# Three changes of tile form and order around the attention scores of a hybrid block

## The chip, the cores and the metric

The kernel runs on one core of one Trainium2 chip. Its time is the device time of one execution in microseconds, given as the median over runs. A profile is one execution taken by the hardware profiler, with every instruction of every engine: TensorE (PE, with its weight loads PEld), VectorE (DVE), ScalarE (ACT), GpSimd (POOL), and the DMA queues, which SP and others issue.

## The reference

Input x is 8 batches of 512 tokens of 1024 features, all float32. Four residual steps follow each other, each on a layer norm of x:

```python
x = x + attn_a(layernorm(x))   # 32 heads of 32: softmax(q k^T / sqrt(32)) v, then the output product
x = x + ffn(layernorm(x))      # dense 1024 x 1024, rows and tokens gated by clusters that are hit
x = x + attn_b(layernorm(x))   # 4 heads of 256, sigmoid scores, causal
x = x + ffn(layernorm(x))      # the same dense layer again
```

The change touches only the first step, `attn_a`:

```python
qkv = x @ attn_qkvw + attn_qkvb
scores = einsum('bhqd,bhkd->bhqk', q, k) * scale
probs = softmax(scores)
ctx = einsum('bhqk,bhkd->bhqd', probs, v)
return ctx @ attn_ow + attn_ob
```

## The kernel before

`softmax_attention` works through 64 units `n`: 8 batches (`b`) by 8 groups (`g`) of 4 heads. The 4 heads of a group have 32 features each and so fill the 128 partitions. A unit has these steps, each cut in 4 tiles of 128 queries or keys:

- `rows_step` (L863 to L872) computes the scores by query of the next unit, one matmul for each head on its 32 partitions, and VectorE takes the negative maximum of every query (`nmax`, L872).
- `split_max` splits -max into three bf16 parts, and `turn_max` (L884 to L892) turns them with an identity on TensorE; ScalarE copies the result to `shift`, in bf16.
- `keys_step` (L894 to L906) computes the scores by key. It first adds up k times q (L900) and then ones times `shift` (L903) in the same PSUM tile, which subtracts the maximum; ScalarE's exponential (L905) reads that tile into `pT`.
- `values_step` (L918 to L929) multiplies `pT` with v in column tiles of 32, and `normalize` (L931) divides by the sums.

The scores by query and by key share one PSUM tile `sc` of four banks, one bank for each head, in a pool with a single buffer. So each waits until VectorE or ScalarE has read the one before.

What fills TensorE between these steps are the *fillers*: the projections to q, k and v of the unit after next (`project_pieces`), the output products of the batch before (`out_pair`), and transposes and logits for the step that follows. They lie in one queue (`Filler`); each piece has a weight, and `take` runs a share of what is queued. The order of all of TensorE's instructions is thus written out when the program is built, and nothing is reordered by a scheduler. The loop of a unit is

```python
for i in range(TPB):
    rows_step(n + 1, i)
    between()
    if i == 0:
        turn_max(n)
        between()
    keys_step(n, i)
    # i == 0: values_step(n - 1, 1), logits, normalize(n - 1);  i == 2: values_step(n, 0)
    between(False, HD_A if i in (0, 2) and n > 0 else 2 * HD_A)
```

A filler's products go through `product` (L550), which cuts the 128 columns of the stationary operand in column tiles of `width[0]`. `between` sets that width: 64, or 32 where attention values, which use tiles of 32 columns, come just before. `turn_max` and the second step of the cluster logits call `product` too. The first four `rows_step` calls stand ahead of the loop, among products of full width.

A matmul's tile form is written as rows*columns: 32*128 is a tile of 32 rows of the array and all its columns, 128*64 one of all rows and half the columns. Tiles of one form that do not overlap can work side by side.

Of the kernel before, what the change touches and what calls it, by code (L numbers as in the profile page):

```python
# [22 lines left out]
P = 128  # L23
# [6 lines left out]
HEADS_A, HD_A = 32, 32  # L30
# [376 lines left out]
def softmax_attention(tc, cst, stage, filler, clusters, pools, dr, late, args):  # L407
# [11 lines left out]
    nc, small, ps_m = tc.nc, stage.small, stage.ps_m  # L419
# [128 lines left out]
    width = [P]  # L548

    def product(out, lhsT, rhs, **flags):  # L550

        for j in range(P // width[0]):
            cols = ts(j, width[0])
            nc.tensor.matmul(out[cols], lhsT[:, cols], rhs, **flags)  # L554

    first_w = {}
# [36 lines left out]
    def first_pieces(n):  # L593
# [4 lines left out]
        def qk(t, c):  # L598
            def go():
                if c == 0:  # L600
                    st["acc"] = ps_m.tile([P, S], F32, tag="mm", name="mm")
                product(
                    st["acc"], first_w[t, g, c // half][:, c % half, :], xTs[0][:, c, :],
                    start=(c == 0), stop=(c == NC - 1),
                )
                if c == NC - 1:
                    o = st["qk"[t]] = qkpool.tile([P, S], F32, tag=f"qk{t}", name=f"qk{t}_{n}")
                    bias = qkvb_s[:, t * NC + g : t * NC + g + 1]
                    if t == 0:
                        nc.vector.tensor_scalar(o, st["acc"], bias, None, ALU.add)  # L610
                    else:
                        nc.scalar.activation(o, st["acc"], AF.Identity, bias=bias)

            return go

        def v(i, k):
            def go():
                if i == 0 and k == 0:
                    st["acc"] = ps_m.tile([P, TPB, P], F32, tag="mm", name="mm")
                for c in range(half):  # L620
                    product(
                        st["acc"][:, i, :], xTs[0][:, k * half + c, ts(i, P)], first_w[2, g, k][:, c, :],
                        start=(k == 0 and c == 0), stop=(k == 1 and c == half - 1),
                    )
                if i == TPB - 1 and k == 1:
                    st["v"] = vpool.tile([P, TPB, P], F32, tag="v", name=f"v_{n}")
                    nc.scalar.copy(st["v"], st["acc"])

            return go
# [21 lines left out]
    def project_pieces(n):  # L651
# [9 lines left out]
        def qk(k, c0):  # L661
            def go():
                if c0 == 0:
                    st["acc"] = ps_m.tile([P, 2 * P], F32, tag="mm", name="mm")
                for c in (c0, c0 + 1):
                    product(
                        st["acc"], weights.tiles[base + EARLY.index(k)][:, c, :], left(k)[:, c, :],
                        start=(c == 0), stop=(c == half - 1),
                    )
                if c0:  # L670
                    if k == 0:
                        for t in range(2):
                            st["qk"[t]] = qkpool.tile([P, S], F32, tag=f"qk{t}", name=f"qk{t}_{n}")
                    q, kk = st["q"], st["k"]
                    bias = [qkvb_s[:, t * NC + g : t * NC + g + 1] for t in range(2)]
                    gather(nc, k, st["acc"], q[:, lo], kk[:, lo], q[:, hi], kk[:, hi], bias, early=True)
                    weights.done(base + EARLY.index(k))

            return go
# [183 lines left out]
    def rows_step(n, qt):  # L863

        st = state[n]
        if qt == 0:
            st["nmax"] = small.tile([P, TPB, GH], F32, tag="nmax", name=f"nmax_{n}")
        sc = ps_s.tile([P, GH, S], F32, tag="sc", name="sc")
        for h in range(GH):
            rows = ts(h, HD_A)  # L870
            nc.tensor.matmul(sc[:, h, :], st["q"][rows, ts(qt, P)], st["k"][rows, :], start=True, stop=True)  # L871
        nc.vector.tensor_reduce(st["nmax"][:, qt, :], sc, AX.X, ALU.max, negate=True)  # L872

    def split_max(n):
# [19 lines left out]
    def keys_step(n, kt):  # L894

        st = state[n]
        sc = ps_s.tile([P, GH, S], F32, tag="sc", name="sc")
        for h in range(GH):
            rows = ts(h, HD_A)
            nc.tensor.matmul(sc[:, h, :], st["k"][rows, ts(kt, P)], st["q"][rows, :], start=True, stop=False)  # L900
        for h in range(GH):
            rows = ts(h, HD_A)
            nc.tensor.matmul(sc[:, h, :], cst.ones_h[rows, :], st["shift"][rows, :], start=False, stop=True)  # L903
        pT = ptp.tile([P, GH, S], F32, tag="pT", name=f"pT_{n}_{kt}")
        nc.scalar.activation(pT, sc, AF.Exp, scale=SCALE_A)  # L905
        st["pT", kt] = pT  # L906
# [40 lines left out]
        nc.vector.tensor_tensor(out, st["av"], rden, ALU.mult)  # L947
        nc.scalar.activation(out, out, AF.Identity, bias=qkvb_s[:, 2 * NC + g : 2 * NC + g + 1])

    places = [0]  # L950

    def between(sides=True, form=2 * HD_A):


        if sides:
            for _ in range(-(-len(side) // places[0])):
                side.popleft()()
            places[0] -= 1
        width[0] = form
        filler.take()  # L960

    def mix_tile(near, wait):
        norm, logits = tiles.popleft()(blocks=wait)
        filler.mix(norm[:2], 0 if near else 2, 2 if near else 5)
        filler.mix(norm[2:], 9 if near else 14, 3)
        if wait:
            waiting.append(logits)
        else:
            filler.mix(logits, 16 if near else 22, 4)
# [25 lines left out]
    for i in range(TPB):  # L995
        rows_step(0, i)
        run(pieces[6 * i : 6 * i + (6 if i < 3 else len(pieces))])
# [4 lines left out]
    for n in range(units):  # L1002
# [33 lines left out]
        for i in range(TPB):  # L1036
            if n + 1 < units:
                rows_step(n + 1, i)
            if i == 0 and n > 0:
                sum_step(n - 1, TPB - 1)  # L1040
# [4 lines that stand above are left out]
            if i == TPB - 1:  # L1045
                sum_step(n, i - 1)
            keys_step(n, i)
            if i == 1:
                sum_step(n, i)
            if i == 0 and n > 0:  # L1050
                values_step(n - 1, 1)
                if ready:
                    by_cluster, by_token = ready.popleft()
                    run([by_cluster])
                    filler.mix([by_token], 6, 1)
                normalize(n - 1)
            if i == 2:
                values_step(n, 0)
            between(False, HD_A if i in (0, 2) and n > 0 else 2 * HD_A)
# [268 lines left out]
def block_body(tc, long, dr, args, out):  # L1328
# [7 lines left out]
    def pools(stack, side):  # L1336
# [12 lines left out]

    late = [[] for _ in range(TPB)]  # L1350
    attention = softmax_attention(
        tc, cst, stage, filler, hits1, (pools(a_outer, left), pools(a_inner, right)), dr, late,
        (x, xT_in, qkvw, qkvb, ow, ob),
# [319 lines left out]
```

## Time and profile before

| | |
|---|---|
| time, median of 3 runs | 3769.76 us (3768.65 to 3769.84) |
| time of the profiled execution | 3769.5 us |
| its span, first to last instruction | 3767.8 us |
| granted TensorE clock, mean | 0.997 |
| mean DMA rate | 159 GB/s |
| scores by query, L871 | 2048 matmul records, 291.9 us busy |
| scores by key, L900 and L903 | 2048 and 1024 records, 292.9 and 101.1 us busy |
| attention stage with the changed code | from about 40 to about 2560 us |

The span is what the trace shows; the time of an execution has under 2 us around it. Busy time of TensorE counts a record from its start to an end that is modelled, so neighbouring records overlap: the starts of records are firmer than their lengths. A float32 matmul leaves two matmul records and two weight loads, a bf16 one leaves one of each.

### The profile page before, as it was taken

What the parts mean: (1) busy time and instruction counts of PE and PEld (TensorE: products, weight loads), DVE (VectorE), ACT (ScalarE), POOL (GpSimd) and SP (SyncE); (2) the same over time, 40 slices, a digit from 0 to 9 for tenths busy, and PEclk for the clock granted to TensorE, in tenths of its full rate; (3) what the DMA queues carried; (4) which work ended last, traced back from release to release, by engine and by line L of the source; (5) the groups of instructions that cost most, each with busy time, mean ns of one, the idle gap of its engine ahead of it and who ended that gap; (6) DMA issues with size and microseconds to landing.
All of it is one profiled execution on the core that took longest, in us unless ns stands there. A gap on an engine that the chain in (4) does not pass through costs nothing.

```text
span 3767.8 us, 72200 instructions
## 1 busy us (share of the span) xinstructions
PE 3716.6 (99%) x30746; PEld 1902.9 (51%) x30746; DVE 2543.7 (68%) x3495; ACT 909.8 (24%) x983; POOL 594.0 (16%) x572
## 2 busy tenths in 40 slices
PE   8999999999999999999999999998999999999999
PEld 4444455554545555555545445443444467764444
DVE  4777676777667667766766767665788845556656
ACT  1222222222222222222222322222111144430000
POOL 1222111111111111111111111111000045530000
PEclk9999999999999999999999999999999999999999
DMA  5335444645655455465455444346566667763332
GB/s 171 115 127 168 142 137 146 194 137 150 188 144 152 149 160 168 132 194 151 134 179 163 141 148 123 118 155 235 159 178 173 170 190 233 226 210 128 134 128 101
DMA packets 728625, 598.29 MB, mean 159 GB/s; under 512 B 322152, under 2 KB 574064, under 8 KB 728304
## 3 DMA queue, kind: packets, MB, share of 16 engines
q1 hardware_dynamic: 701072, 496.40, 46.0%
q0 software_dynamic: 22912, 81.54, 5.6%
q10 hardware_dynamic: 4320, 15.73, 1.0%
q8 instruction: 243, 3.98, 0.4%
q14 instruction: 78, 0.64, 0.1%
HBM read 459.30 MB, written 134.25 MB: 158 GB/s over the span
## 4 chain that ended last, share of the span: by engine, by line
PE 90%; DVE 5%; DMA 1%; issue 1%; SPq 1%; POOL 0%; ACT 0%; DVEq 0%; POOLq 0%; ACTq 0%
PE mm L554 41%; PE dense L1236 17%; PE sc L900 7%; PE sc L871 7%; PE av L927 6%; PE o L1314 4%; PE csc L1295 3%; PE sc L903 1%; PE logitsT L325 1%; PE den L939 1%; DVE nmax L872 1%; PE tp L277 1%; DVE sum L916 0%; SPq L300 0%; DVE u L142 0%
## 5 line engine op out<-in xcount | busy, mean ns | idle before, releaser
L872 DVE TENSOR_REDUCE nmax<-sc 128x4 f32<-128x2048 f32 x256 | 585.9, 2289 | 294.7 <-PE sc L871 294.7
L905 ACT ACTIVATE pT<-sc 128x2048 f32<-128x2048 f32 x256 | 480.8, 1878 | 1151.8 <-PE sc L903 1146.9
L914 POOL TENSOR_TENSOR sum<-pT,pT 128x1024 f32<-128x1024 f32 x128 | 309.8, 2442 | 766.1 <-ACT pT L905 724.9
L554 PE MATMUL mm<-xT,w 128*64 128x256 f32 (+1 forms) x3736 | 429.0, 383 | 1.2 <-DVE rden L942 1.2
L554 PEld LDWEIGHTS mm<-xT,w 128*64 128x64 f32 (+1 forms) x3736 | 241.8, 135 | 197.1 <-issue 47.1
L554 PE MATMUL mm<-s,w 128*32 128x256 f32 (+1 forms) x3672 | 321.2, 381 | 0.5
L900 PE MATMUL sc<-qk,qk 32*128 32x512 f32 x2048 | 292.9, 641 | 10.5 <-DVE nmax L872 9.8
L916 DVE TENSOR_TENSOR sum<-sum,pT 128x2048 f32<-128x2048 f32 x128 | 291.9, 2280 | 1.0 <-ACT pT L905 1.0
L871 PE MATMUL sc<-qk,qk 32*128 32x512 f32 x2048 | 291.9, 640 | 0.4 <-ACT pT L905 0.3
L142 DVE TENSOR_TENSOR u<-dense,u 128x512 f32<-128x512 f32 x223 | 149.1, 685 | 186.9 <-PE dense L1236 170.2
L554 PEld LDWEIGHTS mm<-s,w 128*32 128x32 f32 (+1 forms) x3672 | 180.4, 122 | 176.0 <-issue 68.0
L554 PE MATMUL mm<-ow,ctxT 128*32 128x512 f32 (+2 forms) x1276 | 246.6, 599 | 0.4 <-DMA ow<-o_T 0.4
L927 PE MATMUL av<-pT,v 128*32 128x512 f32 x2048 | 246.6, 599 | 0.0
L1236 PE MATMUL dense<-sum,s 128*128 128x512 f32 x512 | 232.1, 594 | 2.6 <-DVE s L1183 2.6
L554 PEld LDWEIGHTS mm<-w,xT 128*64 128x64 f32 (+1 forms) x3888 | 197.5, 133 | 57.3 <-issue 44.7
L554 PE MATMUL mm<-w,xT 128*64 128x128 f32 (+1 forms) x3888 | 218.1, 274 | 0.0
L144 DVE SCALAR_TENSOR_TENSOR qk<-mm,qkvb_s,qk 128x256 f32<-128x256 f32 x224 | 107.5, 480 | 130.2 <-PE mm L554 125.1
L1236 PE MATMUL dense<-wT_s,dT_b 128*128 128x512 f32 x384 | 173.1, 598 | 1.7 <-DMA dT_b<-xT 1.7
L554 PE MATMUL mm<-ow,c 128*64 128x512 f32 (+2 forms) x864 | 170.8, 597 | 2.7 <-DMA ow<-o_T 2.7
L1236 PE MATMUL dense<-wT_s,dT_a 128*128 128x512 f32 x384 | 171.0, 593 | 0.0
L554 PE MATMUL mm<-w,s 128*64 128x128 f32 x2688 | 162.5, 274 | 0.0
L1236 PEld LDWEIGHTS dense<-sum,s 128*128 128x128 f32 x512 | 96.4, 190 | 123.4 <-issue 112.1
(231 smaller groups left out, 4504.7 us busy)
## 6 DMA issues: line engine op xcount, KB each, us to landing
w<-in_qkvw SPq DMA_DIRECT2D x252, 256.0 KB, 3.0
ow<-o_T SPq DMA_DIRECT2D x240, 256.0 KB, 3.6
w<-qk_T SPq DMA_DIRECT2D x224, 256.0 KB, 2.7
ow<-in_ow SPq DMA_DIRECT2D x180, 256.0 KB, 3.1
w<-v_T SPq DMA_DIRECT2D x112, 256.0 KB, 2.7
x<-in_x SPq DMA_DIRECT2D x32, 512.0 KB, 5.3
dT_a<-xT SPq DMA_DIRECT2D x32, 512.0 KB, 6.1
x_a<-x SPq DMA_DIRECT2D x32, 512.0 KB, 6.8
```

Source lines behind the costliest of these rows:

```text
L142: nc.vector.tensor_tensor(out, acc, other, ALU.add)
L554: nc.tensor.matmul(out[cols], lhsT[:, cols], rhs, **flags)
L871: nc.tensor.matmul(sc[:, h, :], st["q"][rows, ts(qt, P)], st["k"][rows, :], start=True, stop=True)
L872: nc.vector.tensor_reduce(st["nmax"][:, qt, :], sc, AX.X, ALU.max, negate=True)
L900: nc.tensor.matmul(sc[:, h, :], st["k"][rows, ts(kt, P)], st["q"][rows, :], start=True, stop=False)
L905: nc.scalar.activation(pT, sc, AF.Exp, scale=SCALE_A)
L914: nc.gpsimd.tensor_tensor(st["sum"][:, h, :], st["pT", 0][:, h, :], st["pT", 1][:, h, :], ALU.add)
L916: nc.vector.tensor_tensor(st["sum"], st["sum"], st["pT", kt], ALU.add)
L927: nc.tensor.matmul(st["av"][rows, :], st["v"][:, kt, rows], pT[:, h, :], start=(kt == 0), stop=(kt == TPB - 1))
L1236: nc.tensor.matmul(st["acc"], st["left"][LEFT[k]][:, c, :], self.w[RIGHT[k]][:, c, :], start=(c == 0), stop=(c == half - 1),)
L1295: nc.tensor.matmul(sc[:, AT_OFF[i] : AT_OFF[i] + n], k[:, c, ts(i, P)], xT[:, c, i * P :], start=(c == 0), stop=(c == 1),)
L1314: nc.tensor.matmul(acc[:, j - jj, :], at[:, start : start + P], self.v[b * TPB + i][:, cols], start=(i == 0), stop=(i == j),)
```

## The change

It has three parts. In `rows_step` each head's matmul is cut in two, for 64 queries each, so that the scores by query use tiles of 32 rows by 64 columns, eight to a step. In `keys_step` the ones times `shift` product comes first and opens the accumulation, and k times q comes second and closes it. And each call of `between` puts a 32 in the list `opening` before it takes fillers; the first call of `product` takes it out and cuts its columns in four tiles of 32, all further products have the width as before. The list is cleared at the end of the call, so `turn_max`, which is called between two of them, is not touched.

```diff
     def product(out, lhsT, rhs, **flags):
 
-        for j in range(P // width[0]):
-            cols = ts(j, width[0])
+
+        w = opening.pop() if opening else width[0]
+        for j in range(P // w):
+            cols = ts(j, w)
             nc.tensor.matmul(out[cols], lhsT[:, cols], rhs, **flags)
...
         for h in range(GH):
             rows = ts(h, HD_A)
-            nc.tensor.matmul(sc[:, h, :], st["q"][rows, ts(qt, P)], st["k"][rows, :], start=True, stop=True)
+            for j in range(2):
+                cols = ts(2 * qt + j, P // 2)
+                nc.tensor.matmul(sc[ts(j, P // 2), h, :], st["q"][rows, cols], st["k"][rows, :], start=True, stop=True)
         nc.vector.tensor_reduce(st["nmax"][:, qt, :], sc, AX.X, ALU.max, negate=True)
...
         for h in range(GH):
             rows = ts(h, HD_A)
-            nc.tensor.matmul(sc[:, h, :], st["k"][rows, ts(kt, P)], st["q"][rows, :], start=True, stop=False)
+            nc.tensor.matmul(sc[:, h, :], cst.ones_h[rows, :], st["shift"][rows, :], start=True, stop=False)
         for h in range(GH):
             rows = ts(h, HD_A)
-            nc.tensor.matmul(sc[:, h, :], cst.ones_h[rows, :], st["shift"][rows, :], start=False, stop=True)
+            nc.tensor.matmul(sc[:, h, :], st["k"][rows, ts(kt, P)], st["q"][rows, :], start=False, stop=True)
...
-    places = [0]
+    places, opening = [0], []
 
     def between(sides=True, form=2 * HD_A):
...
         width[0] = form
+        opening[:] = [HD_A]
         filler.take()
+        opening.clear()
```

## The prediction

> **What bounds the kernel now.** I read first the page's busy times, then its chain of work that ended last, then the timeline of TensorE inside the attention stage, and last the weight loads kept apart by shape.
>
> From the page, part 1 (busy time, share of the span, instructions) and part 4 (the chain):
>
> ```profile
> PE 3716.6 (99%) x30746; PEld 1902.9 (51%) x30746; DVE 2543.7 (68%) x3495; ACT 909.8 (24%) x983; POOL 594.0 (16%) x572
> ...
> PE 90%; DVE 5%; DMA 1%; issue 1%; SPq 1%; POOL 0%; ACT 0%; DVEq 0%; POOLq 0%; ACTq 0%
> ```
>
> TensorE is busy 99% of the span and is 90% of the chain. No other engine has to be made faster or kept from being slower: what a stretch of TensorE's stream gains or loses, the span gains or loses. So the question is what lies between the matmuls. The timeline of TensorE over one piece of the attention loop (start, length, line, tiles, tile form, records):
>
> ```profile
> 1508.20 1.14 PE L871 MATMUL sc<-qk,qk 32*128 32x512 f32 x8
> 1509.27 1.95 PE L554 MATMUL mm<-xT,w 128*64 128x256 f32 x16
> 1511.05 0.39 PE L554 MATMUL tpm<-ident_h,parts 128*64 128x128 bf16 x8
> 1511.27 1.90 PE L554 MATMUL mm<-xT,w 128*64 128x256 f32 x16
> 1513.10 1.14 PE L900 MATMUL sc<-qk,qk 32*128 32x512 f32 x8
> 1514.06 0.39 PE L903 MATMUL sc<-shift,ones_h 32*128 32x512 bf16 x4
> 1514.39 1.92 PE L927 MATMUL av<-pT,v 128*32 128x512 f32 x16
> ...
> 1530.43 3.67 PE L554 MATMUL mm<-s,w 128*64 128x256 f32 x32
> 1534.04 1.14 PE L900 MATMUL sc<-qk,qk 32*128 32x512 f32 x8
> ```
>
> The form (128*64) is rows by columns of one tile of the array. An f32 matmul leaves two records, a bf16 one leaves one. The tiles of a form run side by side, so I count in rounds, one record on every tile. Single starts in the trace (1509.537, 1509.753, 1509.969) put rounds of 256 f32 columns 0.216 us apart; rounds of 512 take 0.427, and of 512 in bf16 0.213. What a segment takes beyond its rounds sits at a change of form:
>
> - 128*64 from the scores into the turned maxima, which have the same form: 1511.05 - 1509.27 = 1.78 for 8 rounds (1.726). So entering costs 0.054.
> - 128*64 from the turned maxima into scores: 1513.10 - 1511.27 = 1.83 for 8 rounds. So leaving costs 0.104. Check: 16 rounds with both ends take 1534.04 - 1530.43 = 3.61 = 3.453 + 0.054 + 0.104.
> - 32*128, scores by query: 1509.27 - 1508.20 = 1.07 for 2 rounds of 0.427, over 0.216: the second round starts 0.534 after the first, so 0.107 is entering and 0.109 leaving.
>
> Entering follows the columns of one weight load, which nothing hides there: 0.107 for 128 columns, 0.054 for 64; for 32 the starts of the attention values give 0.026. Leaving is about 0.10 whatever follows. The place that matters most is one of the few where one column form follows another:
>
> ```profile
> 87.55 1.92 PE L927 MATMUL av<-pT,v 128*32 128x512 f32 x16
> 89.40 1.08 PE L554 MATMUL mm<-xT,w_first 128*64 128x512 f32 x4
> 90.31 1.04 PE L554 MATMUL mm<-wv,xT 128*64 128x128 f32 x16
> ```
>
> 89.40 - 87.55 = 1.85 for 4 rounds (1.71): 0.14, as much as where rows change. The last round starts at 88.861 and the next form at 89.403, 0.115 beyond a round, and its second round 0.053 late at 89.883. Four places in the trace leave 32 columns for 64 at this price. Going from 32 to 64 columns is therefore not free.
>
> **The change, part by part**
>
> **1. The first filler product in four column tiles.** Each call of between() with a form of 64 now starts with one product of 32, followed by 64 again. The streaming is the same (half as wide, twice as many side by side). Inserted is one more segment: enter 0.026, leave 0.115, together 0.141 us. The 64-column segment behind it still pays its own 0.054. Going through the trace's records I count 252 such places behind scores by query and 130 behind scores by key or values (the other 126 run at 32 already). 382 x 0.141 = 53.9 us. Behind the turned maxima it is worse: today that stretch goes on in the same form with nothing to pay. There the 64 segment is cut in two: 0.141 + 0.104 + 0.054 = 0.299, x 64 = 19.1. Sum 73.0. At four of these places another form follows anyway, which takes off about 1: **+71.8**. All of it is on TensorE's path; nothing covers it, since the engine waits there for itself. Bounds: above, 73; below, if the second switch were free, the narrower entry would gain 382 x 0.027 = 10 us. The row at 89.40 decides for the upper end.
>
> **2. -max first in scores by key.** Today the f32 weights of k (128 columns) are loaded in the open, 0.107, and the bf16 ones behind them under a running round. Turned round, the ones are loaded in the open and k under the ones' round of 0.213, which is longer than 0.107. The loads of both shapes:
>
> ```profile
> L900 PEld LDWEIGHTS sc<-qk,qk 32*128 32x128 f32 x2048 | 80.2, 183 | 126.8 <-issue 55.9 <-DVE nmax L872 31.8 <-DVE qk L142 14.9
> ...
> L903 PEld LDWEIGHTS <-ones_h 32*128 32x128 bf16 x1024 | 28.9, 93 | 57.7 <-issue 57.7
> L325 PEld LDWEIGHTS logitsT<-nT,cT_s 128*32 128x32 f32 x1024 | 28.3, 110 | 20.8 <-issue 17.3 <-ACT nT L279 3.3
> ```
>
> The mean of one is 183 ns for f32 and 93 for bf16, less than the 110 of a 32-column f32 load, whose entry is 0.026. A load met in the open shows 181 ns, so 88 ns go: 256 x 0.088 = **-22.5**. The Trainium skill, "TensorE: Matmul & The Clock Gate", section "LDWEIGHTS (loading the stationary operand)", lets a load grow with its columns alone (columns / 1.2 in ns): 107 ns for both, and this edit would gain nothing. Its section on Fast Weight Load has 128 non-FP32 weights load about twice as fast as measured: 53 ns, a gain of 13.7. I take the row. Bounds 0 and -24. What is new is that the segment waits for the shift (ScalarE, L892) one f32 part, 0.96 us, earlier. From the end of that cast to the start of L900 there are 0.70 us in nearly every unit; once, at the end of attention, it is 0.17 short. Who releases L900 today:
>
> ```profile
>   DVE nmax L872: 41.6, 46
> ...
>   ACT shift L892: 0.8, 1
> ```
>
> So no wait is added; the buffer of the scores is freed by the same reduction as before, and the exponential behind still starts after the last matmul of the step.
>
> **3. Scores by query in tiles of 32 by 64.** 256 steps go from 4 tiles to 8: 2048 more matmul records, as many loads, the same two rounds. No row shows this form. Entering should be that of 64 columns: -0.053. But records of one round start 0.0067 apart (1508.199, 1508.206, 1508.213, 1508.219), and the last of eight starts 0.047 in, not 0.020: +0.027. Net -0.026 x 256 = **-6.7**. The Trainium skill's same page, section on packing small matmuls, gives about 4 ns per tile; the sum would be -9.5. Bounds: -13.6 (no stagger), +6.9 (the two loads of a row group one after the other), and +218 if the two column tiles of a row group do not run side by side (one more 0.427 per round). The Trainium skill, "TensorEngine Tiling (Array Packing)", section "Available Configurations", lists 32x64 as eight independent tiles, and both splits are seen side by side separately (four 32*128, two 128*64), so I take the first.
>
> Sum: 71.8 - 22.5 - 6.7 = +42.6 on the profiled execution of 3769.5 us (span 3767.8), 0.3 under the median of the runs, 3769.76: **3812**. No DMA, SP or GpSimd instruction is moved; VectorE's reduction starts when the scores end, as now.
>
> **The rivals**
>
> - *Column forms switch freely within one product's accumulation.* The inserted segment then gains 10 instead of costing 72: -10 - 22.5 - 6.7 = -39, 3730, faster. For it: every place that I price is between different products. Against: 89.40 above. It decides below 29.2 / 446 = 0.065 us for each opening, against 0.161 in my sum.
> - *The eight tiles run as two fours.* 42.6 + 218: about 4030. Against it the two splits above; for it only that no trace here has this form.
> - *The weight side gives nothing.* Loads of one row group in turn (+13.6) and no gain from the ones (+22.5): 3848 with both, 3826 or 3835 with one.
> - *The change does not do what it says*: the first filler piece is seldom a product. Then -29, 3740. The records speak against it: each of the 446 places has one.
>
> **How the numbers follow.** My sum with its small variations 0.80, the weight side failing in full 0.06, two fours 0.07, free switching or an opening that does not bite 0.07. The range runs from 3794 (rows and ones at their best ends, some openings cheaper) to 3842 (the ones gain nothing, rows a little more). 0.2%, 7.5 us, is about what a measurement of this kernel can tell from none: faster 0.06, same 0.02, slower 0.92.
>
> **What would show it.** Step 1: 128*32 segments of 8 records (4 tiles, 2 rounds) right behind L871, 0.57 for 256 columns before the 128*64 starts (0.432 + 0.141). Step 2: L903 ahead of L900, from 1.28 to about 1.20 from the first start to the next form. Step 3: L871 with 4096 records and 1.04 to the next form; 1.9 would mean two fours. Records on PE 30746 + 2048 + 446 x 4 = 34578. A 128*32 to 128*64 step without its 0.11, or a wait for the shift, would make me wrong.

## The result, and the profile after

The changed kernel takes 3803.1 us (median of 4 runs, 3801.1 to 3804.3) against 3769.8 for the kernel before: ratio 1.0088, 95% interval 1.007 to 1.0105. It is slower by 33 us; the forecast was 42 us slower. The two profiled spans are 34.8 us apart (3802.6 and 3767.8).

From the page, the same two parts as before: busy times, and the chain that ended last.

```profile
PE 3751.6 (99%) x34594; PEld 1833.6 (48%) x34594; DVE 2544.5 (67%) x3495; ACT 909.7 (24%) x983; POOL 594.1 (16%) x572
...
PE 93%; DVE 3%; DMA 1%; issue 1%; SPq 1%; ACT 0%; POOL 0%; DVEq 0%; ACTq 0%; POOLq 0%
```

TensorE still carries the chain, now 93% of it. Its records went from 30746 to 34594. That is 16 more than the 34578 expected, or four openings at 4 records each: 450 products are opened, not 446, the last four in the last unit, where no scores by query stand ahead. The same piece of the attention loop in TensorE's timeline follows (start, length, line, tiles, form, records). A line of this view takes in all neighbours of one source line and tile name under the form of the first, so x20 here is one product of 8 records at 128*32 and three of 4 records at 128*64:

```profile
1530.30 1.11 PE L875 MATMUL sc<-qk,qk 32*64 32x512 f32 x16
1531.34 2.08 PE L556 MATMUL mm<-xT,w 128*32 128x256 f32 x20
1533.26 0.39 PE L556 MATMUL tpm<-ident_h,parts 128*64 128x128 bf16 x8
1533.58 2.08 PE L556 MATMUL mm<-xT,w 128*32 128x256 f32 x20
1535.60 0.39 PE L904 MATMUL sc<-shift,ones_h 32*128 32x512 bf16 x4
1535.82 1.03 PE L907 MATMUL sc<-qk,qk 32*128 32x512 f32 x8
1536.78 1.92 PE L931 MATMUL av<-pT,v 128*32 128x512 f32 x16
```

Read start to start, beside the piece of before:

| | before | after | difference |
|---|---|---|---|
| scores by query to the next form | 1.07 | 1531.34 - 1530.30 = 1.04 | -0.03 |
| filler, 8 rounds, up to the turned maxima | 1.78 | 1533.26 - 1531.34 = 1.92 | +0.14 |
| turned maxima to the next filler | 0.22 | 1533.58 - 1533.26 = 0.32 | +0.10 |
| filler, 8 rounds, up to scores by key | 1.83 | 1535.60 - 1533.58 = 2.02 | +0.19 |
| scores by key to the attention values | 1.29 | 1536.78 - 1535.60 = 1.18 | -0.11 |

The inserted 32-column segment costs 0.14 behind the scores and 0.29 (0.10 + 0.19) behind the turned maxima. Weight loads, kept apart by shape:

```profile
L907 PEld LDWEIGHTS sc<-qk,qk 32*128 32x128 f32 x2048 | 101.7, 185 | 4.5
...
L875 PEld LDWEIGHTS sc<-qk,qk 32*64 32x64 f32 x4096 | 59.6, 129 | 112.5 <-issue 93.3 <-ACT pT L909 16.9 <-ACT qk L614 1.2
...
L904 PEld LDWEIGHTS <-ones_h 32*128 32x128 bf16 x1024 | 26.2, 91 | 124.9 <-issue 121.2 <-DVE nmax L876 3.6
```

The loads of k (L907) have almost no idle time before them any more, 4.5 us where it was 126.8: they now run under the round of the ones. The ones, a load of 91 ns, stand in the open instead.

For a sum over the whole attention stage I split TensorE's stream of one profiled execution, from start to start up to the last scores, into three parts:

- Rounds at their nominal length, 0.427 us for 512 f32 columns, half of that in bf16, and in proportion for fewer columns. They make 2306.7 us in every kernel here.
- Form changes: each change counted at the price seen in the starts. Entering costs 0.106, 0.053 and 0.0265 for 128, 64 and 32 columns in f32, and 0.013 for the ones. Each further tile of a round adds 0.0067, or 0.0034 with the ones. Leaving costs 0.091 from a form of 32 rows and 0.0955 from one of all rows.
- The rest: late starts, more than 0.03 us behind what rounds and prices give, and a few nanoseconds for each round that has another of its form on either side.

| kernel | median us | form changes | rest | of it late starts |
|---|---|---|---|---|
| before | 3769.8 | 190.8 | 47.6 | 26.0 |
| after | 3803.1 | 230.1 | 43.3 | 24.1 |
| opening only | 3832.9 | 263.1 | 44.9 | 26.0 |
| max first only | 3747.7 | 164.4 | 53.5 | 31.3 |
| 32x64 only | 3765.8 | 184.0 | 50.6 | 29.0 |
| scores only | 3742.7 | 157.7 | 55.0 | 32.9 |
| three openings | 3953.7 | 388.0 | 33.9 | 19.4 |
| none behind the turned maxima | 3788.1 | 211.2 | 46.3 | 26.3 |
| all 32 | 3746.7 | 152.1 | 65.2 | 43.6 |
| full-width opening | 3869.4 | 299.3 | 41.4 | 22.6 |
| rows 32x32 | 3756.3 | 164.6 | 61.2 | 37.2 |
| more filler first | 3773.5 | 157.7 | 85.7 | 63.8 |
| before, light VectorE | 3758.7 | 190.8 | 39.8 | 18.4 |
| scores only, light VectorE | 3728.2 | 157.7 | 41.9 | 20.2 |

The column of form changes is a count times a price, so agreement of a theory with it is no test by itself. Two things test it. The prices hold place by place: in the changed kernel's trace at the 442 places where 64 columns follow 32 without idle time, the next form starts 0.0957 us (median) beyond the last round, nine in ten between 0.0953 and 0.0967. And the rest stays between 34 and 65 in all kernels but one, while form changes range from 152 to 388. The rest is that of one execution each; times of the kernel before alone spread from 3766.3 to 3774.0 over 25 runs, so a difference of 2 us in it may be chance.

After minus before: form changes +39.3, rest -4.3, together +35.0, against 34.8 in the spans. Of the -4.3, 1.9 are late starts; the other 2.4 are the few nanoseconds of rounds, which the rounds at the ends of the added segments do not pay. Every kernel below is compared with runs of the kernel before on the same chip, whose medians were 3768.2 to 3769.3.

### The profile page after: what moved, and what is told of

Same layout as the page of the kernel before. It is cut to its first block, busy times and chain, and to the rows that moved or that the text cites. A ratio compares the mean times of both kernels' runs of the same rounds, so it can differ in the third digit from the quotient of the medians.

```text
span 3802.6 us, 79896 instructions
## 1 busy us (share of the span) xinstructions
PE 3751.6 (99%) x34594; PEld 1833.6 (48%) x34594; DVE 2544.5 (67%) x3495; ACT 909.7 (24%) x983; POOL 594.1 (16%) x572
## 4 chain that ended last, share of the span: by engine, by line
PE 93%; DVE 3%; DMA 1%; issue 1%; SPq 1%; ACT 0%; POOL 0%; DVEq 0%; ACTq 0%; POOLq 0%
PE mm L556 43%; PE dense L1242 18%; PE sc L875 7%; PE av L931 6%; PE sc L907 6%; PE o L1320 4%; PE csc L1301 3%; PE sc L904 2%; PE logitsT L325 1%; PE den L943 1%; PE tp L277 1%; DVE nmax L876 0%; DMA cx<-x 0%; PE tpm L556 0%; SPq L300 0%
## 5 line engine op out<-in xcount | busy, mean ns | idle before, releaser
L556 PE MATMUL mm<-xT,w 128*64 128x256 f32 (+1 forms) x4408 | 455.5, 388 | 0.8 <-DVE rden L946 0.8
L556 PEld LDWEIGHTS mm<-xT,w 128*64 128x64 f32 (+1 forms) x4408 | 218.7, 126 | 258.4 <-issue 121.2
L556 PE MATMUL mm<-s,w 128*32 128x256 f32 (+1 forms) x3908 | 329.2, 382 | 0.0
L875 PE MATMUL sc<-qk,qk 32*64 32x512 f32 x4096 | 285.1, 613 | 0.1
L907 PE MATMUL sc<-qk,qk 32*128 32x512 f32 x2048 | 263.2, 588 | 0.0
L556 PE MATMUL mm<-w,xT 128*64 128x128 f32 (+1 forms) x4112 | 227.1, 276 | 0.0
L556 PE MATMUL mm<-ow,c 128*32 128x512 f32 (+2 forms) x980 | 173.2, 598 | 2.7 <-DMA ow<-o_T 2.7
L556 PE MATMUL mm<-w,s 128*64 128x128 f32 (+1 forms) x2808 | 166.7, 275 | 0.0
L556 PEld LDWEIGHTS mm<-w,s 128*64 128x64 f32 (+1 forms) x2808 | 146.1, 134 | 28.8 <-issue 28.8
```

Source lines behind the costliest of these rows:

```text
L875: nc.tensor.matmul(sc[ts(j, P // 2), h, :], st["q"][rows, cols], st["k"][rows, :], start=True, stop=True)
```

## The experiments

**Each part alone, and the scores without the opening.** Each of the first three runs keeps one part of the change and has the code of before in the other two; the fourth keeps both parts of the scores and has no opening. In the three without an opening, one line of the changed kernel is gone:

```diff
-        opening[:] = [HD_A]
```

> The first filler product in four column tiles alone; scores by query and by key as before. Theory A, a fixed price for each change of form (0.141 us for each of 382 inserted segments, 0.30 for each of the 64 behind the turned maxima): +72 us, 3842, less a few us if the longer fillers take up waits of the scores for the reduction. Theory B, switching between column forms is cheap inside one product's accumulation: under +29, most likely about -10. Theory C, the total of +33 is due to an opening that costs only about 62: 3832, with the scores at their predicted -29.

> Ones times shift ahead of k times q in scores by key, alone. Theory A, the open load is the bf16 one: the changed kernel's trace has 0.117 us of form change in a step where the one before has 0.220, so 256 x 0.103 = -26 us, 3743.5. Rival, the load's time goes by its columns alone: 0, 3770. Rival, a shorter step meets the reduction of the maxima more often and the gain turns into waits ahead of the step: -15 or less, with more idle time of PE before the scores by key.

> Scores by query in 32x64 tiles, alone. Theory A, 0.053 less to enter and 0.027 more for eight starts: 256 x -0.027 = -7 us, 3763. Rival, no effect alone because the form that follows now pays more to come in behind 32x64 than behind 32x128: 0.

> Both changes of the scores, without the opening of the fillers. Theory A, the parts add up: -26 - 7 = -33 us, 3736.5. Rival, waits come back: VectorE's reduction of 2.29 us between scores by query and by key is met sooner in the steps with short fillers, gain under 28, 3742 or more.

Measured: opening only 3832.9 (ratio 1.017, 1.0156 to 1.0183), +64; max first only 3747.7 (0.9943, 0.9931 to 0.9956), -21; 32x64 only 3765.8 (0.999, 0.9983 to 0.9996), -3; scores only 3742.7 (0.9926, 0.9913 to 0.994), -26. Theory B falls: switching column forms inside one product's accumulation is not cheap. The opening alone, with scores as before, shows the changed kernel's 1.92 us for the 8 rounds that took 1.78:

```profile
1551.28 1.14 PE L873 MATMUL sc<-qk,qk 32*128 32x512 f32 x8
1552.35 2.08 PE L556 MATMUL mm<-xT,w 128*32 128x256 f32 x20
1554.27 0.39 PE L556 MATMUL tpm<-ident_h,parts 128*64 128x128 bf16 x8
```

In form changes all four stand where theory A has them, +72.3, -26.4, -6.8 and -33.1. The parts of the scores also show it directly, from the step's first start to the next form: the median of the scores by key falls from 1.287 to 1.183 with -max first, and the mean of the 256 steps by query from 1.071 to 1.044 with 32x64. But the times do not follow in full: of the scores' 33 us some 7 come back as rest (47.6 to 55.0), as the rival of the last run had it. The time of 32x64 alone, 1.5 to 6.4 us under the kernel before, lies between its two theories, so there the trace decides and not the time. Theory C's time for the opening alone, 3832, came out for another reason: its form changes are 72, not 62, with -2.7 of rest in the profiled execution, which was the slowest of that kernel's runs (3837.4).

**More of the suspected price.** Three openings for each stretch, one less where it is dearest, and one of full width:

```diff
-        opening[:] = [HD_A]
+        opening[:] = [HD_A, 2 * HD_A, HD_A]       # three openings
+        opening[:] = [] if again else [HD_A]      # again: the call behind turn_max
+        opening[:] = [P]                          # full width
```

> The changed kernel with three opening products for each call of between: 32, then 64, then 32 columns, then the width of the stretch, behind values too. Theory A, each boundary has its price whatever the product (leave about 0.10 with its stagger, enter 0.053 or 0.027): walking through the sequence of forms gives +198 us over before in form changes, less up to 10 of waits taken up: about 3960. Theory C, the fixed price is partly something else that comes once in a stretch (such as a late first fill of a product): the second and third boundary add less, 3880 or below.

> The changed kernel, but with no opening in the call of between that follows the turned maxima. Theory A: there an opening costs 0.30 each, 64 of them, so 19 us come off: form changes +21 over before, waits about 0 to -3, 3787. Rival, all openings cost the same 0.15: 10 us come off, 3793.

> The changed kernel with the opening product in one piece of 128 columns, behind values (form 32) too. Theory A: entering costs 0.106, leaving 0.095: with the 126 stretches behind values, which now are cut as well, form changes +109 over before, 3873. Rival, a switch between one full tile and column tiles is no change of form that drains: far below, about 3780.

Measured: 3953.7 (1.0492, 1.0477 to 1.0506), 3788.1 (1.0053, 1.0039 to 1.0067) and 3869.4 (1.027, 1.0256 to 1.0284), within 7 us of theory A each time and far from the rivals of the first and last. The middle run's time does not tell its theories apart, as its interval reaches to 3793.6, the rival's value; its span is 16.2 us under the changed kernel's with 3.0 more of rest, which fits 19 better than 10. One stretch with three openings in TensorE's timeline:

```profile
1615.05 2.37 PE L556 MATMUL mm<-xT,w 128*32 128x256 f32 x24
1617.26 0.39 PE L556 MATMUL tpm<-ident_h,parts 128*64 128x128 bf16 x8
1617.58 2.37 PE L556 MATMUL mm<-xT,w 128*32 128x256 f32 x24
1619.88 0.40 PE L904 MATMUL sc<-shift,ones_h 32*128 32x512 bf16 x4
```

It is the same 8 rounds (four products, 32, 64, 32 and 64), and takes 1617.26 - 1615.05 = 2.21 where one opening took 1.92 and none 1.78: +0.14 for the first, +0.29 for the next two boundaries. So the price belongs to each boundary, also between full and column tiles. The times lie 12 us and 8 us below the form changes in the first and last because the rest falls to 33.9 and 41.4. About half of that are late starts (26.0 to 19.4 and 22.6): longer fillers take up waits. The other half are the few nanoseconds of rounds that now stand at the ends of segments.

**Narrower everywhere.** If 32 columns are cheaper to enter, and a boundary is what costs, all fillers of the loop can be 32 wide, with no boundary among them:

```diff
-    def between(sides=True, form=2 * HD_A):
+    def between(sides=True, form=HD_A):
...
-            between(False, HD_A if i in (0, 2) and n > 0 else 2 * HD_A)
+            between(False, HD_A)
...
-    width[0] = 2 * HD_A
+    width[0] = HD_A
```

> The scores as changed, no opening, and every filler of the attention loop, the turned maxima included, in four tiles of 32 columns. Theory A: every entry behind scores falls from 0.053 to 0.027, but the last of four tiles starts 0.013 later than the last of two, net -0.013 for some 420 entries: -5.6 us against the scores alone, 3737. Rival, four tiles for each round cost something inside the rounds, or the 64-column forms hide their loads better: no gain or a loss, 3743 or more.

It took 3746.7 (0.9947, 0.9934 to 0.9959), no better than the scores alone. The form changes fell by 5.6 as theory A has it (157.7 to 152.1), but the rest rose by 10.2. All of that are late starts (32.9 to 43.6) and nothing is inside the rounds, so the rival has the time and not the reason. This program has 46610 matmul records, 42% more than the scores alone, and TensorE stood idle seven times with nothing that the profile shows to wait for (us, times, longest), which the scores alone do not have:

```profile
PE mm L556 <- issue: 4.8, 7, 2.3
```

That is about half of the 10. What holds TensorE there, and what makes up the others, stays open.

**Sixteen tiles.** The scores by query cut once more:

```diff
-            for j in range(2):
-                cols = ts(2 * qt + j, P // 2)
+            for j in range(4):
+                cols = ts(4 * qt + j, P // 4)
```

> As the scores alone without an opening, but scores by query in sixteen tiles of 32x32. Theory A, the entry falls from 0.053 to 0.027, but the last of sixteen starts 0.10 in, not 0.047: +0.027 for each of 256 steps, +7 us in form changes against the 32x64 version, which cancels all that 32x64 gained: 3749. Rival, starts of tiles do not lengthen a step, only the load counts: -7 us, 3736.

3756.3 (0.9961, 0.9949 to 0.9974), 14 above the scores with 32x64 and 7 above theory A. One step:

```profile
1503.97 1.14 PE L875 MATMUL sc<-qk,qk 32*32 32x512 f32 x32
1505.04 1.95 PE L556 MATMUL mm<-xT,w 128*64 128x256 f32 x16
```

It takes 1.07 again, where 32x64 took 1.04, so the starts of tiles do lengthen a step, and the form changes are up by 6.9 as theory A worked out. Two rounds of 0.427 and both ends still fit into the 1.07, so all sixteen tiles run side by side. Another 6.2 are rest, which I had not expected, and 3.7 us of idle time with nothing shown to wait for are new here as well:

```profile
PE mm L556 <- issue: 3.7, 6, 1.0
```

**Where the 7 us went.** First by moving filler into the stretch that waits:

```diff
-FILLER_SHARES = (0.5, 0.5, 0.6, 1.0, 1.0, 1.0, 0.7, 1.0, 1.0)
+FILLER_SHARES = (0.65, 0.65, 0.6, 1.0, 1.0, 1.0, 0.7, 1.0, 1.0)
```

> As the scores alone without an opening, but with larger shares of the fillers in the first two stretches of a unit (0.65 each, not 0.5), which lie ahead of the first scores by key. Form changes stay at 158 us. Theory D, the waits that took back 5 to 7 us of the gain are those of the first scores by key in units 2 and 4 of each batch for the reduction: with more filler there 3 us or more come back, 3739 or less. Rival, the same work then is missing in a later stretch and the waits move there: 3742 or more.

A miss: 3773.5 (1.0009, 1.0003 to 1.0016), 31 us above the scores alone and all of it rest (55.0 to 85.7). TensorE's longest waits in this run (waiting line, releaser, us, times, longest):

```profile
PE mm L556 <- DVE s L1330: 21.9, 6, 3.7
...
PE sc L904 <- DVE nmax L876: 10.5, 6, 3.6
```

The first line is new. A share moved forward takes products that need VectorE's sums (`s`) before these are made, once in each of six batches. Behind five of these waits the granted clock stands at half for 3.4 us. In the row of one such stretch (busy time of PE, PEld, DVE, ACT and POOL, then clock, DMA share and GB/s) it is the 0.50:

```profile
917.60:921.00 3.40, 3.40 (x20) 1.85 (x20) 1.01 (x3) 0.00 (x0) 0.00 (x0) 0.50 0.02 5
```

Rounds of 0.216 us take 0.43 there. Five stretches in which TensorE is busy nearly throughout cost about half their length, an estimate of 8 us of the 31. The six long waits for the reduction (`nmax`) did not get shorter: 10.5 us, against 10.1 in the scores alone. But with the new waits in it this run is no clean test of theory D; it shows that a filler moved ahead can run into its own operand.

Then by relieving VectorE, with and without the changed scores. These two leave half of the softmax sums out and are for timing alone:

```diff
         else:
-            nc.vector.tensor_tensor(st["sum"], st["sum"], st["pT", kt], ALU.add)
```

> The kernel before, with the 128 additions of 2.28 us by which VectorE adds the third and fourth tile of exponentials to the softmax sums left out (the sums then lack them). It takes 292 us from VectorE's queue and nothing from TensorE's. Theory D, the waits ahead of the scores are for VectorE's reduction, which stands behind other work: of the 27 us of waits in the attention stage some 5 to 10 go, 3760 to 3765. Rival, the waits come from elsewhere (loads, fillers): 3768.

> The scores as changed without an opening, with the same 128 additions left out. Theory D: with VectorE early, nothing of the form changes' 33 us is given back, so this lies 31 to 34 us under the run of the kernel before with the same left out. Rival: the distance stays at 26, as with VectorE's full load.

The kernel before falls to 3758.7 (0.9974, 0.9964 to 0.9985), and the changed scores to 3728.2 (0.9891, 0.9878 to 0.9905): 30.5 apart, where with full load it was 26. The rest is 39.8 and 41.9, only 2.1 apart instead of 7.4. The distance is just under the 31 that theory D asked for; about 2 us of give-back remain without VectorE's additions. So most of what the scores' gain gave back hangs on VectorE's load.

That it is the reduction for which TensorE waits longer, as theory D says, is not shown. TensorE's waits for it are nearly the same with the old and the new scores (us, times, longest), with full load

```profile
PE sc L900 <- DVE nmax L872: 9.8, 6, 2.9
PE sc L904 <- DVE nmax L876: 10.1, 6, 2.9
```

and with the light one:

```profile
PE sc L900 <- DVE nmax L872: 8.0, 6, 3.7
PE sc L904 <- DVE nmax L876: 7.9, 6, 3.2
```

In single starts the late starts of the scores alone come to 6.9 us more than those of the kernel before: 1.2 ahead of the scores by key, 2.8 ahead of fillers (a new line of 1.4 us is for `qk`, a result of VectorE), 1.1 ahead of the turned maxima, and 1.7 in rounds at half the granted clock. The last is partly chance: both kernels wait 2.92 us at one place, and only the scores alone then have a stretch at 0.50, where the kernel before (first pair) stays at 1.00:

```profile
408.95 1.14 PE L900 MATMUL sc<-qk,qk 32*128 32x512 f32 x8 [2.92 <-DVE nmax L872]
408.50:411.90 3.40, 2.95 (x28) 1.58 (x30) 0.99 (x2) 1.49 (x1) 0.00 (x0) 1.00 0.17 59
...
405.83 0.40 PE L904 MATMUL sc<-shift,ones_h 32*128 32x512 bf16 x4 [2.92 <-DVE nmax L876]
406.30:409.70 3.40, 3.40 (x18) 1.24 (x12) 0.08 (x1) 1.85 (x1) 0.00 (x0) 0.50 0.00 0
```

**The better version.** The scores' two changes without the opening are 0.74% faster than the kernel before (3742.7) and 60 us faster than the changed one.

## Why the prediction was right, and what was off

- *TensorE's stream sets the time, and what counts is the change of form.* Shown: form changes carry the sign and nearly the size in the opening's four runs.
- *Step 1, the opening, +71.8.* In form changes it is +72.3 alone, from which 2.7 go for the few nanoseconds of rounds that the openings replace. The price taken from four places between different products holds inside one product's accumulation, and at every opening (450 of them, where I had counted 446). "Column forms switch freely" is ruled out by the opening alone and by three openings.
- *Step 2, -max first, -22.5.* In form changes -26.4: the term was sized 3.9 too small. I took 0.088 from the lengths of two loads; the starts show that the first round of k now begins 0.013 beyond a round of the ones (1535.822 - 1535.596 = 0.226, for 0.213), not 0.107, which is 0.094, and the closing segment leaves after 0.101 instead of 0.111, as its tiles start 0.0034 apart. Loads that grow with columns alone are ruled out (nothing would have come), and so is a factor of two (-13.7): here it is nearer eight. No wait for the shift appeared.
- *Step 3, 32x64, -6.7.* In form changes -6.8, with 8 starts 0.0067 apart and an entry of 0.053; 4 ns for each tile would have given -9.5. "Two fours" is ruled out: 1.04 us for a step.
- *The step that was off: "what a stretch of TensorE's stream gains or loses, the span gains or loses."* I counted waits as unchanged. They are not: 6.9 us came back as late starts when the scores were made shorter, and the medians have the same (33.1 less 25.9). The changed kernel, whose fillers are longer, has 1.9 us less of them, which may be chance. I also let every round keep its few nanoseconds beside the added segments, which is 2.4 us too much. These and step 2 are why +42.6 became +35 in the spans and +33 in the medians: 42.6 less 3.9 (step 2) less 4.3 (1.9 of late starts, 2.4 of rounds), plus 0.6 elsewhere in the form changes. The last 1.5 lie between one execution and the median of runs that spread over 3.

## What to carry to other kernels

Count the changes of tile form in TensorE's stream and price each from the starts of records: leaving plus the weight load that nothing hides. A narrower first product saves 0.027 us of load and costs 0.14, so a form should be chosen for a whole stretch; and what must stand first behind a change should be the operand that loads fastest. Where a stretch of the bottleneck also covers another engine's work, part of what it gains turns into waits there (7 of 33 us in the scores alone), and part of what it loses is taken from them (7 of 197 with three openings).

## What the runs showed of the hardware that I had not expected

A bf16 load of 128 columns into 32-row tiles costs 0.013 us in the open, an eighth of the 0.106 of the f32 load of the same shape, and tiles loaded so start 0.0034 us apart (1535.596, 1535.599, 1535.602, 1535.606) instead of 0.0067. After some waits of 3 to 4 us the granted clock stands at half for 3.4 us, which costs about 1.7 us more (an estimate: half of a busy stretch); after others of the same length it does not. Leaving a form costs 0.09 to 0.10 us beyond the round of its last tile in every pair of forms here, also from 32 columns to 64 in the middle of one accumulation. Sixteen 32x32 tiles in f32 run side by side as eight and four do: two rounds and both ends in 1.07 us.
